# Seven block products in place of eight for the new gate of a GRU, in a graph network on one core

## Chip, cores and metric

One core of one Trainium2 chip. The metric is the device time of one execution in microseconds (us), lower is better; the time of a kernel is the median of its runs.

## What is computed

Four layers run over 128 graphs of 64 nodes with 256 features each, so over 8192 rows. Every layer adds its result to its input (`x = x + layer(relu(layernorm(x)))`). Layers 0 and 1 are graph attention (four heads, then one head), each ending in `elu`. Layer 2 is a relational convolution. Layer 3, where most of the work is, is a gated graph network of three steps:

```
for i in range(3):
    m = h @ weight[i]                      # messages
    a = adjacency applied to m             # sums over neighbours
    gi = a @ w_ih.T + b_ih;  gh = h @ w_hh.T + b_hh
    r = sigmoid(gi_r + gh_r)
    z = sigmoid(gi_z + gh_z)
    n = tanh(gi_n + r * gh_n)
    h = (1 - z) * n + z * h
```

All data are float32. For `r` and `z` the two matrix products may be added before anything else happens. For `n` they may not: `gh_n` is multiplied by `r` first, so its two halves (`gh_n` from h, `gi_n` from a) have to be kept apart.

## The kernel before

**Tiling.** The rows are split into 16 groups of 512 (four pairs of graphs). Features lie on partitions in two blocks of 128 (index `k` for inputs, chunk `c` for outputs), the 512 rows of a group lie along the free axis in two halves `S0` and `S1` of 256. A group passes attention twice, then the relational layer, then `before_recurrence` (layer norm and first neighbour sums), then the recurrence of three steps.

**Order of work.** Nothing runs in the order in which it is written. Class `Plan` records every operation with an assumed cost, the operations it depends on, and a job (`begin(name, start, end)`). `emit` then walks through an assumed time: of the operations that could start earliest on each engine, it takes the one with the earliest due time. The due time comes either from the job's own start and end (in proportion to what is left of the job) or, where the end is None, from the operations that follow. `LATENCY` is the assumed time from an engine's end to another engine's start. The order on each engine is fixed when the kernel is built. The recurrence of group g is due from `start + g * period`, and attention of later groups is fitted in between. In the first 115 us of the assumed time, waits of TensorE are filled with products of constants (`spare`, line 1315, into the bank `ni`).

**The recurrence** (`recurrence`, `class Chunk`). The products for `r` and `z` of one chunk use a scheme of seven block products where the plain way has eight (two input blocks by two output blocks by two halves of rows). It needs sums of weight blocks (`weight_sums`, made once into `wsum`) and sums of state blocks (`state_sums`, three or four POOL additions for each of h and a, into `hS` and `aS`). `mul(name, q, source)` is product number q from h (source 0) or a (source 1); it multiplies 128 x 128 weights with 256 columns. Products 1, 6, 5 and 3 are added up one after another in the PSUM bank `ry`. Between them ACT copies the partial sums that other outputs need (`m1_there`, `m16_there`, `m165_there`), so TensorE can't go on in that bank until the copy is done. Product 2 goes to `rm`, products 7 and 4 to `rz`. DVE adds those banks to the copies, ACT applies tanh (sigmoid is written with tanh).

**The n gate before.** `gate("nh", k)` and `gate("ni", k)` are plain: for each chunk two products of 512 columns into bank `nh` (from h) and two into `ni` (from a), eight for each step. ACT takes `nh` out with its bias into `t` (`nh_there`, 512 columns), DVE makes `(r + 1) * t` (`r_there`), then adds `ni` from PSUM (`n_there`), ACT applies tanh, POOL forms `d = h - n`, DVE finishes `d = (z + 1) * d` and `hnew = d / 2 + n` (`h_there`).

**After a step**, `back` transposes the new state on TensorE, `along` multiplies with the adjacency in 64 x 64 tiles, `state_sums` follows.

**Attention.** `values` takes the value columns out of PSUM on ACT and the few attention terms `es` on DVE; `aggregate_graphs` scales the result on DVE; `elu_add` takes the minimum with 0 on DVE and the exponential on ACT. Each has a switch `by_scalar` that gives the work to ACT; it is off for all groups (`g < 0`). `later_weights` prepares the weights of layers 2 and 3 in the early part, job "weights". All compute instructions are recorded by one helper, so in the profile they all have line 384 (line 605 where many products are one operation, `beside`).

PSUM has the banks `ry`, `rm`, `rz`, `nh` and `ni` of one tile each, which only the recurrence uses, and three for everything else (`mt` in the code; in the early part the first four of the five are lent out as well).

Of the kernel before, what the change touches and what calls it, by code (L numbers as in the profile page):

```python
# [8 lines left out]
F32 = mybir.dt.float32  # L9
I32 = mybir.dt.int32  # L10
AF = mybir.ActivationFunctionType
ALU = mybir.AluOpType
# [187 lines left out]
class Job:  # L200
# [3 lines left out]
    def __init__(self, start, end, after):  # L204
        self.start, self.end, self.after, self.left, self.length = start, end, after, 0, 0.0


class Plan:
# [3 lines left out]
    LATENCY = 164.2  # L212
# [54 lines left out]
    def emit(self):  # L267
# [20 lines left out]
        for op in reversed(self.ops):  # L288
            if op.job.end is None:
                op.due = min((t.due for t in op.then), default=1e9) - op.cost  # L290
            else:
                op.due = (op.job.end - (op.job.end - op.job.start) * op.tail / op.job.length) * 1e3
# [148 lines left out]
def kernel(  # L441
# [54 lines left out]
    wsum = nc.kept(const, [P, 1 + LAYERS, 3, D], F32, name="wsum")  # L496
    bi = nc.kept(const, [P, 6], F32, name="bi")
# [224 lines left out]
    def weight_sums(w, ws):  # L722

        r0, r1, z0, z1 = w[:, 0, :D], w[:, 1, :D], w[:, 0, D : 2 * D], w[:, 1, D : 2 * D]
        nc.gpsimd.tensor_tensor(ws[:, 0], z0, z1, ALU.add)
        nc.gpsimd.tensor_tensor(ws[:, 1], ws[:, 0], r0, ALU.subtract)
        nc.gpsimd.tensor_tensor(ws[:, 2], r1, ws[:, 1], ALU.subtract)
        nc.gpsimd.tensor_tensor(z0, r0, z0, ALU.subtract)

# [27 lines left out]
    def recurrence(work, psum, start, src, abd, store, in_parts=False):  # L757
# [16 lines left out]
        class Chunk:  # L774
# [3 lines left out]
            def __init__(self, c, i, hT, hnew):  # L778
                self.c, self.i, self.hT, self.hnew = c, i, hT, hnew
                self.banks, self.started = {}, set()  # L780
                self.r, self.t, self.z, self.d = (work.tile([P, T], F32, name=name) for name in "rtzd")
# [8 lines left out]
            def mul(self, name, q, source):  # L790

                w, m, ms = ((whh, self.hT, hS), (wc[:, self.i], aT, aS))[source]
                ws = wsum[:, (0, 1 + self.i)[source]]
                cs = slice(self.c * P, (self.c + 1) * P)
                zs = slice(D + self.c * P, D + (self.c + 1) * P)
                lhsT, rhs = {
                    1: (w[:, 0, cs], m[:, 0, S0]),
                    2: (w[:, 1, cs], m[:, 1, S0]),
                    3: (ws[:, 2, cs], m[:, 1, S1]),
                    4: (w[:, 1, zs], ms[:, 3]),  # L800
                    5: (ws[:, 0, cs], ms[:, 0]),
                    6: (ws[:, 1, cs], ms[:, 1]),
                    7: (w[:, 0, zs], ms[:, 2]),
                }[q]
# [4 lines left out]
                return 0.43  # L809

            def both(self, name, q):
                return self.mul(name, q, 0) + self.mul(name, q, 1)

            def gate(self, name, k):

                w, m = {"nh": (whh, self.hT), "ni": (wc[:, self.i], aT)}[name]
                ps, new = self.bank(name)
                f = 2 * D + self.c * P
                nc.tensor.matmul(ps, w[:, k, f : f + P], m[:, k, :], start=new, stop=not new)
                return 0.86  # L820

            def nh_there(self):
                nc.scalar.activation(self.t, self.banks["nh"], AF.Identity, bias=bh[:, 4 + self.c : 5 + self.c])

            def r_there(self, h):

                r, t = self.r[:, h], self.t[:, h]
# [6 lines left out]
                nc.vector.scalar_tensor_tensor(t, r, 1.0, t, op0=ALU.add, op1=ALU.mult)  # L834

            def n_there(self, h):
                t = self.t[:, h]
                nc.vector.tensor_tensor(t, t, self.banks["ni"][:, h], ALU.add)
                nc.scalar.activation(t, t, AF.Tanh, bias=bi[:, 4 + self.c : 5 + self.c])
                nc.gpsimd.tensor_tensor(self.d[:, h], self.hT[:, self.c, h], t, ALU.subtract)  # L840
# [16 lines left out]
            def h_there(self, h):  # L857
                d = self.d[:, h]
                nc.vector.scalar_tensor_tensor(d, self.z[:, h], 1.0, d, op0=ALU.add, op1=ALU.mult)
                nc.vector.scalar_tensor_tensor(  # L860
                    self.hnew[:, self.c, h], d, 0.5, self.t[:, h], op0=ALU.mult, op1=ALU.add
                )

        for i in range(LAYERS):
            last = i == LAYERS - 1
            hnew = work.tile([P, K, T], F32, name="hT")
            a = Chunk(0, i, hT, hnew)

            a.mul("ry", 1, 0)
            a.gate("nh", 0)  # L870
            if i > 0:
                aT = work.tile([P, K, T], F32, name="aT")
                if 0:
                    back(hT, hnat, 1)
                    along(psum, hnat, abd, aT, range(K))
                else:
                    along(psum, hnat, abd, aT, [0])
                state_sums(aT, aS, 0)
            a.mul("ry", 1, 1)
            a.m1_there()  # L880
            a.gate("ni", 0)
            if i > 0 and not 0:
                back(hT, hnat, 1)
            a.gate("nh", 1)
            a.nh_there()
            if i > 0:
                if not 0:
                    along(psum, hnat, abd, aT, [1])
                state_sums(aT, aS, 1)
            a.mul("rm", 2, 0) + a.mul("rz", 7, 0)  # L890
            a.mul("rm", 2, 1)
            a.r_there(S0)
            a.mul("rz", 7, 1)
            a.gate("ni", 1)
            a.n_there(S0)
            a.both("ry", 6)
            a.m16_there()
            b = Chunk(1, i, hT, hnew)
            b.both("rm", 2)
            a.both("ry", 5)  # L900
            a.m165_there()
            a.z_there(S1)
            b.gate("nh", 0)
            a.both("ry", 3)
            a.r_there(S1)
            a.n_there(S1)
            a.h_there(S1)
            a.both("rz", 4)
            a.z_there(S0)
            a.h_there(S0)  # L910

            b.gate("nh", 1)
            b.nh_there()
            b.both("ry", 1)
            b.m1_there()
            b.r_there(S0)
            b.both("rz", 7)
            b.both("ry", 6)
            b.m16_there()
            b.gate("ni", 0)  # L920
            b.both("ry", 5)
            b.m165_there()
            b.z_there(S1)
            hnat = work.tile([P, G, D], F32, name="hnat")
            back(hnew, hnat, 0, src if last else None)
            b.both("ry", 3)
            b.r_there(S1)
            b.gate("ni", 1)
            b.n_there(S0)
            b.n_there(S1)  # L930
            b.h_there(S1)
            b.both("rz", 4)
            b.z_there(S0)
            b.h_there(S0)
# [13 lines left out]
    with ExitStack() as s1:  # L948
# [148 lines left out]
        def attention(g, p0, n, layer, heads, we, pool):  # L1097
# [4 lines left out]
            wv, es = values(pool, psum, src, heads, we, g >= AHEAD, True, g < 0)  # L1102
# [51 lines left out]
            o = aggregate_graphs(pool, psum, t, wv, heads, g < 0)  # L1154
            elu_add(pool, src, o, nc.vector if g < 1 else nc.gpsimd, g < 0)
# [5 lines left out]
        def later_weights(prep):  # L1161
# [7 lines left out]
            weight_sums(whh, wsum[:, 0])  # L1169
            ihT = prep.tile([P, K, 3 * D], F32, name="ihT", tag="hhn")  # L1170
            transpose_blocks(psum, ihT, ihn, 6)
            for i in range(LAYERS):
# [12 lines left out]
                weight_sums(wc[:, i], wsum[:, 1 + i])  # L1185
# [49 lines left out]
        gru = Pool(None, 1, ("r3", "t3", "z3", "d3"))  # L1235
# [19 lines left out]
        nc.begin("weights", 18.0, 79.1)  # L1255
        later_weights(early)
        layers = (first_layer, second_layer, third_layer)
        start, period = 93.6, 83.8
# [274 lines left out]
```

## Time and profile before

| what | value |
|---|---|
| time, median of 3 runs | 1435.51 us (1435.34 to 1436.21) |
| the profiled execution, its own time | 1434.47 us |
| its span, first to last instruction | 1432.5 us |
| share of clock granted to TensorE | 0.998 |
| TensorE busy (matmul) / weight load | 1412.5 us / 973.6 us |
| DVE / ACT / POOL busy | 1041.5 / 778.7 / 597.7 us |
| first product of the recurrence starts | 113.0 us |
| last product that isn't of the recurrence starts | 1324.9 us |

How to read it. PE is TensorE (matmul), PEld its weight loads, DVE is VectorE, ACT is ScalarE, POOL is GpSimd. A float32 matmul instruction leaves two records in the trace, so "x384" matmul records are 192 products. A group is named "output tile <- input tiles". Matmul durations reach from the start to the end of the pipeline and overlap each other; the spacing of the starts is what a product costs in a stream. The kernel has a second path (`general`) for inputs out of bounds, which isn't run; its instructions are in the listing but not in the trace.

### The profile page before, as it was taken

The page shows a single profiled execution, that of the slowest core. Times are in us where ns is not written, and L with a number is a line of the kernel's source. Part 1 is how long each engine was busy: PE and PEld are TensorE (multiplying, and loading weights), DVE is VectorE, ACT ScalarE, POOL GpSimd, SP SyncE. Part 2 cuts the span into 40 slices and gives each one's busy share as a digit, 9 for nine tenths or more (in the row PEclk, how much of TensorE's full clock was granted, in tenths as well). Part 3 has the DMA queues.
Part 4 walks back from the last instruction along what each step waited for, and adds up shares of the span by engine and source line. Part 5 has one row for each costly group of instructions (what it writes and reads, how often), then busy time and mean ns, then how long its engine had stood idle before and what let it go on. Part 6 is the DMA issues. An engine that isn't in the chain of part 4 may idle for free.

```text
span 1432.5 us, 28063 instructions
## 1 busy us (share of the span) xinstructions
PE 1412.5 (99%) x9779; PEld 973.6 (68%) x9779; DVE 1041.5 (73%) x2745; ACT 778.7 (54%) x1853; POOL 597.7 (42%) x744
## 2 busy tenths in 40 slices
PE   9999999999999999999999999999999999999997
PEld 9676676666667666666766666676666667666664
DVE  5568688686867878686887868688686868774544
ACT  3654655555565565556555555655655555554543
POOL 1424624534434453443445344344534434452422
PEclk9999999999999999999999999999999999999999
DMA  7010221222223122222312222231212222110000
GB/s 214 19 27 24 38 60 30 47 53 52 60 43 75 28 51 54 52 60 44 77 25 51 54 52 60 43 76 27 46 39 48 46 42 58 25 34 15 16 16 18
DMA packets 299421, 67.91 MB, mean 47 GB/s; under 512 B 274696, under 2 KB 297480, under 8 KB 299272
## 3 DMA queue, kind: packets, MB, share of 16 engines
q1 hardware_dynamic: 298712, 65.50, 21.7%
q8 instruction: 81, 1.33, 0.4%
q10 hardware_dynamic: 560, 0.52, 0.1%
q14 instruction: 68, 0.56, 0.1%
HBM read 28.06 MB, written 8.53 MB: 26 GB/s over the span
## 4 chain that ended last, share of the span: by engine, by line
PE 88%; DVE 4%; SPq 3%; ACT 3%; DMA 1%; issue 1%; POOL 1%; DVEq 0%; POOLq 0%; ACTq 0%
PE ry L384 22%; PE mm L384 16%; PE rz L384 11%; PE ni L384 11%; PE nh L384 10%; PE rm L384 5%; PE tp L384 4%; PE mm L605 3%; SPq L384 3%; PE tp L605 2%; PE ni L1315 2%; DVE d L384 1%; POOL d L384 1%; DVE hT L384 1%; DMA t<-row 1%
## 5 line engine op out<-in xcount | busy, mean ns | idle before, releaser
L384 POOL TENSOR_TENSOR d<-hT,t 128x256 f32<-128x256 f32 x192 | 151.9, 798 | 487.7 <-ACT t L384 486.8
L384 PE MATMUL ni<-aT,wc 128*128 128x512 f32 x384 | 194.1, 592 | 0.0
L384 PE MATMUL nh<-hT,whh 128*128 128x512 f32 x384 | 193.8, 593 | 0.2 <-DVE hT L384 0.2
L384 ACT ACTIVATE z<-z,brz 128x256 f32<-128x256 f32 x192 | 97.4, 507 | 155.9 <-DVE z L384 155.3
L384 DVE SCALAR_TENSOR_TENSOR d<-z,d 128x256 f32<-128x256 f32 x192 | 127.2, 669 | 58.1 <-POOL d L384 45.2
L384 POOL TENSOR_TENSOR hS<-hT 128x256 f32<-128x256 f32 x96 | 73.9, 770 | 175.5 <-PE ry L384 136.3
L384 ACT COPY z<-ry 128x256 f32<-128x256 f32 x192 | 71.2, 371 | 126.4 <-PE ry L384 91.2
L384 DVE SCALAR_TENSOR_TENSOR t<-r,t 128x256 f32<-128x256 f32 x192 | 98.0, 511 | 50.2 <-ACT r L384 44.5
L384 DVE TENSOR_TENSOR z<-rz,z 128x256 f32<-128x256 f32 x192 | 80.2, 418 | 59.1 <-PE rz L384 46.6
L384 PE MATMUL rz<-hS,whh 128*128 128x256 f32 x384 | 119.5, 393 | 1.1 <-DVE z L384 1.0
L384 PE MATMUL mm<-wl,hT 128*128 128x512 f32 x248 | 118.1, 598 | 0.0
L384 PE MATMUL ry<-hS,wsum 128*128 128x256 f32 x384 | 115.9, 383 | 0.8 <-ACT z L384 0.8
L384 PE MATMUL rz<-aS,wc 128*128 128x256 f32 x384 | 115.6, 383 | 0.0
L384 PE MATMUL ry<-aS,wsum 128*128 128x256 f32 x384 | 114.2, 379 | 0.0
L384 ACT ACTIVATE hn<-xg,var,rstd 128x256 f32<-128x256 f32 x200 | 107.1, 592 | 9.9 <-DVE var L384 9.8
L384 ACT ACTIVATE t<-t,bi 128x256 f32<-128x256 f32 x192 | 93.8, 502 | 19.8 <-DVE t L384 19.2
L384 PEld LDWEIGHTS ry<-hS,wsum 128*128 128x128 f32 x384 | 70.0, 190 | 47.0 <-issue 32.0
L384 DVE BATCH_NORM_STATS2 st<-xg 128x6 f32<-128x256 f32 x256 | 98.5, 413 | 3.2 <-DMA xg<-in_x_dram 2.5
L384 DVE SCALAR_TENSOR_TENSOR hT<-d,t 128x256 f32<-128x256 f32 x192 | 91.9, 485 | 6.1
L384 POOL TENSOR_TENSOR rstd<-var,mhalf 128x4 f32<-128x4 f32 (+1 forms) x70 | 68.7, 984 | 56.4 <-DVE var L384 47.4
L384 PEld LDWEIGHTS nh<-hT,whh 128*128 128x128 f32 x384 | 70.1, 190 | 27.3 <-issue 17.4
L384 PEld LDWEIGHTS ry<-aS,wsum 128*128 128x128 f32 x384 | 73.0, 190 | 22.7 <-issue 10.3
(203 smaller groups left out, 3227.6 us busy)
## 6 DMA issues: line engine op xcount, KB each, us to landing
hT<-hn SPq DMA_DIRECT2D x896, 32.0 KB
xg<-in_x_dram SPq DMA_DIRECT2D x15, 512.0 KB
out_dram<-hnat SPq DMA_DIRECT2D x15, 512.0 KB
t<-row SPq DMA_DIRECT2D x28, 256.0 KB
at<-in_adj_dram SPq DMA_DIRECT2D x64, 32.0 KB
eg<-in_adj_dram SPq DMA_DIRECT2D x64, 32.0 KB
ag<-in_adj_dram SPq DMA_DIRECT2D x16, 128.0 KB
t<-row SPq DMA_DIRECT2D x28, 64.0 KB
```

Source lines behind the costliest of these rows:

```text
L384: return do(*[real(a) for a in args], **{k: real(v) for k, v in kwargs.items()})
L605: nc.nc.tensor.matmul(*[real(x) for x in product], start=True, stop=True)
L1315: nc.spare = lambda: nc.nc.tensor.matmul(pause, warm, warm, start=True, stop=True)
```

## The change

1. **n by seven products.** The new function `part_of_n` makes both chunks of `gh_n` (source 0) or of `gi_n` (source 1) from seven products of 256 columns, 14 for each step. The two chunks take the place that the r and z blocks have in `Chunk`, with their own weight sums `nsum`. Products 1, 6, 5 and 3 go to bank `nh` with ACT copies in between, 2 to `rm`, 7 and 4 to `ni`, and DVE adds (`plus`) the latter three times. Source 0 ends in `t`, source 1 in `hnew`, except that chunk 0, half S1 of source 1 is read from PSUM.
2. **The gate arithmetic** follows (`gate_n`): `tc` plus `hnew` are mostly two SBUF operands; the difference h - n goes into `hnew` and no longer into an own tile `d`. `r`, `z`, `t` are now tiles of both chunks.
3. **Order in which a step is written:** neighbour sums, `part_of_n(0)`, r of chunk 0, `part_of_n(1)`, then n, z, the new state and `back` of chunk 0, then the same of chunk 1.
4. **ACT** takes `es`, the scaling of the one-head attention and elu's minimum (as `Relu(-x)`, `Exp(-x)`) for all groups (`g < 16`).
5. **The plan:** `LATENCY` 164.2 to 177.99; jobs without an end get due times by `spread * (cost + LATENCY)`; "weights" and all jobs of groups 0 and 1 have no end now; `start`, `period` and due times move a little; the filling of waits stops when the first recurrence bank is taken.

The core of the diff:

```diff
-    LATENCY = 164.2
+    LATENCY = 177.99
...
-                op.due = min((t.due for t in op.then), default=1e9) - op.cost
+                op.due = 1e9
+                for t in op.then:
+                    late = 0.0 if t.engine == op.engine else self.LATENCY
+                    op.due = min(op.due, t.due - op.job.spread * (op.cost + late))
...
+    nsum = nc.kept(const, [P, 1 + LAYERS, 3, P], F32, name="nsum")
...
-            def gate(self, name, k):
-
-                w, m = {"nh": (whh, self.hT), "ni": (wc[:, self.i], aT)}[name]
-                ps, new = self.bank(name)
-                f = 2 * D + self.c * P
-                nc.tensor.matmul(ps, w[:, k, f : f + P], m[:, k, :], start=new, stop=not new)
-                return 0.86
...
+        def part_of_n(source, i, hT, to):
+
+            w, m, ms = ((whh, hT, hS), (wc[:, i], aT, aS))[source]
+
+            def mul(ps, q, start, stop):
+                lhsT, rhs = operands(q, w, nsum[:, (0, 1 + i)[source]], *NN, slice(0, P), m, ms)
+                nc.tensor.matmul(ps[:, S0], lhsT, rhs, start=start, stop=stop, skip_group_check=True)
+
+            def there(c, h, ps):
+                if source == 0:
+                    nc.scalar.activation(to[:, c, h], ps[:, S0], AF.Identity, bias=bh[:, 4 + c : 5 + c])
+                else:
+                    nc.scalar.copy(to[:, c, h], ps[:, S0])
+
+            def plus(c, h, ps):
+                engine = nc.vector if source == 0 else nc.vector
+                engine.tensor_tensor(to[:, c, h], ps[:, S0], to[:, c, h], ALU.add)
+
+            y = psum.tile([P, T], F32, name="nh")
+            mul(y, 1, True, False)
+            there(0, S0, y)
+            m2 = psum.tile([P, T], F32, name="rm")
+            mul(m2, 2, True, True)
+            plus(0, S0, m2)
+            mul(y, 6, False, False)
+            there(1, S0, y)
+            m7 = psum.tile([P, T], F32, name="ni")
+            mul(m7, 7, True, False)
+            mul(y, 5, False, False)
+            there(1, S1, y)
+            plus(1, S1, m7)
+            mul(m7, 4, False, True)
+            plus(1, S0, m7)
+            mul(y, 3, False, True)
+            return y
...
+            def gate_n(c, h, y):
+                tc, new = t[:, c, h], hnew[:, c, h]
+                nc.vector.scalar_tensor_tensor(tc, r[:, c, h], 1.0, tc, op0=ALU.add, op1=ALU.mult)
+                nc.vector.tensor_tensor(tc, tc, y[:, S0] if (c, h) == (0, S1) else new, ALU.add)
+                nc.scalar.activation(tc, tc, AF.Tanh, bias=bi[:, 4 + c : 5 + c])
+                nc.gpsimd.tensor_tensor(new, hT[:, c, h], tc, ALU.subtract)
...
-            wv, es = values(pool, psum, src, heads, we, g >= AHEAD, True, g < 0)
+            wv, es = values(pool, psum, src, heads, we, g >= AHEAD, True, g < 16)
...
-            o = aggregate_graphs(pool, psum, t, wv, heads, g < 0)
-            elu_add(pool, src, o, nc.vector if g < 1 else nc.gpsimd, g < 0)
+            o = aggregate_graphs(pool, psum, t, wv, heads, g < 16)
+            elu_add(pool, src, o, nc.vector if g < 1 else nc.gpsimd, g < 16)
...
-        nc.begin("weights", 18.0, 79.1)
+        nc.begin("weights", 18.0, 0 or None)
...
-        start, period = 93.6, 83.8
+        start, period = 84.23, 83.53
...
-                    nc.begin((g, p0, i), at[i], at[i + 1], [users[i]] if i in users and not spare else [])
+                    end = None if g < 2 else at[i + 1]
+                    nc.begin((g, p0, i), at[i], end, [users[i]] if i in users and not spare else [])
...
-            nc.spare = lambda: nc.nc.tensor.matmul(pause, warm, warm, start=True, stop=True)
+            nc.spare = lambda: psum.early and nc.nc.tensor.matmul(pause, warm, warm, start=True, stop=True)
```

## The prediction

> **What bounds the kernel now.** I began with the first part of the page and the chain of waits, which ask the same question from two sides: which engine is never free, and whose work the end hangs on.
>
> ```profile
> PE 1412.5 (99%) x9779; PEld 973.6 (68%) x9779; DVE 1041.5 (73%) x2745; ACT 778.7 (54%) x1853; POOL 597.7 (42%) x744
> ...
> PE 88%; DVE 4%; SPq 3%; ACT 3%; DMA 1%; issue 1%; POOL 1%; DVEq 0%; POOLq 0%; ACTq 0%
> ```
>
> TensorE is busy for 99% and 88% of the last-ending chain is its products. A busy matmul row alone proves little, since its bars overlap, so I looked at starts in the timeline of some steady microseconds.
>
> ```profile
> 300.20 0.60 PE L384 MATMUL rz<-hS,whh 128*128 128x256 f32 x2
> 300.63 0.59 PE L384 MATMUL rz<-aS,wc 128*128 128x256 f32 x2
> 301.06 0.27 PE L384 MATMUL tp<-ident,hT 128*128 128x128 f32 x1
> 301.17 1.02 PE L384 MATMUL nh<-hT,whh 128*128 128x512 f32 x2
> 302.03 0.59 PE L384 MATMUL ry<-hT,whh 128*128 128x256 f32 x2
> ```
>
> A product of 256 columns is followed 0.43 us later by the next, one of 512 columns (301.17 to 302.03) 0.86 us later, whatever tile follows. By the start times of the whole trace the medians are 0.431 and 0.859 us. Both are streams without a hole. The three stretches of the span, cut at the first product of the recurrence and at the last one of another layer, show where that holds:
>
> ```profile
> 0.00:113.00 113.00, 110.94 (x842) 85.96 (x842) 66.85 (x240) 56.81 (x151) 36.14 (x61) 1.00 0.31 83
> 113.00:1325.00 1212.00, 1207.55 (x8342) 823.43 (x8338) 923.42 (x2388) 671.97 (x1590) 523.80 (x633) 1.00 0.23 47
> 1325.00:1432.50 107.50, 93.98 (x608) 64.20 (x600) 51.19 (x118) 49.94 (x113) 37.74 (x51) 0.97 0.07 17
> ```
>
> After the length come PE, PEld, DVE, ACT and POOL. In the middle PE has 4.5 us of 1212 free; DVE, next, is at 76%. At the end, where only the last recurrence is left, PE lacks some 13 us. At the start PE looks busy but a third of that is filling:
>
> ```profile
> L1315 PE MATMUL ni<-warm 128*128 128x128 f32 x318 | 41.7, 286 | 1.1 <-DVE warm L1313 1.1
> L384 PE MATMUL ni<-aT,wc 128*128 128x512 f32 x384 | 194.1, 592 | 0.0
> L384 PE MATMUL nh<-hT,whh 128*128 128x512 f32 x384 | 193.8, 593 | 0.2 <-DVE hT L384 0.2
> ```
>
> 318 records are 159 filling products of 0.22 us, 35 us. The other two rows are the products that the change replaces. So: TensorE's own work sets the time, except in about 35 us of early waits and some 13 us at the end.
>
> **What the Trainium skill says.** "Perfetto Trace Analysis", section "Identifying the Most-Contended Engine", warns that matmul busy time is not a measure of how full TensorE is, because matmuls are pipelined. This trace agrees: bars of 592 ns mean, starts 429 ns apart; therefore I price by starts. "TensorE: Matmul & The Clock Gate", section "Back-to-back issue gap", gives N/2.4 + 2.5 ns warm. With N twice the float32 columns that is 215.8 and 429.2 ns for one record; the medians here are 215.5 and 429.2. So halving a product halves its price, with 2 ns lost, and the shorter one isn't held up by its weight load (190 ns). "SBUF — State Buffer", section "SBUF: two separate sides", says that a DVE instruction with two SBUF inputs and a POOL instruction exclude each other for a whole instruction. The trace agrees: `t<-r,t` takes 384 ns at least and 954 at most between 600 and 700 us.
>
> **Part 1, products.** Removed for each of 48 steps (16 groups by 3): eight products of 512 columns, 8 x 0.859 = 6.87 us. Added: 14 of 256, 14 x 0.431 = 6.03 us. In all 384 x 0.859 = 329.8 against 672 x 0.431 = 289.6: **-40.1 us** of TensorE. Since PE is full before and after in the middle stretch, all of it is on the path there. At the end the chain of the last recurrence decides in part, so a share of 3 of the 48 steps, 2.5 us, could be lost. Switches between 64-row and 128-row products, which cost PE some 0.1 to 0.3 us each, are 324 in both built orders: nothing.
>
> **Part 2, turns of a bank.** New are the copies between products in `nh`, twice per step. TensorE must not write on before ACT has read. Queued behind such a product on PE is everything else, as the order is fixed. What a turn takes is seen near the end: the last product into `ry` before one starts at 1419.26, its second record 0.22 later at 1419.48, and the next product in that bank at 1420.32, 0.84 us after that record's start, of which 0.22 are its own stream: 0.62 with a copy of 371 ns. An evacuation with bias (about 466 ns, from `r<-ry,brz`) gives 0.72. It costs nothing when other products lie in between. In the built order of after, nine of ten turns of `nh` have 1.29 us or more of other products between them, so the cover is mostly there. But all banks together have 191 revisits with under 1.0 us of cover, against 106 before, and the lines of the PE listing with a wait grow from 1829 to 2162 (18%). In the trace of before, what 128-row records took beyond the stream adds up to 29 us between 120 and 1340. Growing with the waits that is +5, growing with the thin revisits (+80%) +24. I take **+8**, nearer to the first, because most thin revisits still have 0.4 us or more of cover. If the cover were gone: see the third rival.
>
> **Part 3, DVE.** Gone: 192 `t<-t,ni` x 0.412 = 79; 124 `es` copies, 18.6; 64 of the one-head `o`, 26.9; `hn<-o`, 31.4. Added: 288 `plus` from PSUM x 0.415 = 119.5; 144 additions of two SBUF operands at the price of `t<-r,t`, 0.511 = 73.6 (425 ns when free, 669 with POOL often in the way); 48 from PSUM, 19.8. Net +57, so 1098 of about 1395 us, 79%. **ACT:** gone 96 x 0.689 = 66; added 192 x 0.466 + 144 x 0.371 + 124 x 0.16 (from copies of 256 and 512 at 371 and 585 ns, extrapolated to a few columns) + 64 x 0.466 + 28 x 1.058 + 8 x 0.632 = 227. Net +161: 940 us, 67%. **POOL** stays: the 192 differences only change their target, and 16 small sums of weights fall into the early part. SP's queue has the same 1254 lines. All of this lies beside TensorE: **0** on the path, price of a lost cover in the second rival. `hnew` is held a little longer than before; three `hT` tiles exist and I price that at 0, with up to 3 us in the range.
>
> **Part 4, early work.** The built order holds 121 filling products for 159, so 38 x 0.22 = 8.4 us fewer, and the first recurrence product follows 54.8 us of 128-row work instead of 71.9; the rest of the weights moves behind it, where it fills waits. But filling now stops at that product, and holes after it aren't seen in the listing. Bounds -9 to +3; I take **-6**. `spread = 3.0` does nothing, as those jobs keep an end.
>
> **Part 5, the end.** After the last r product two plain `ni` products no longer stand before the wait for the new state. Before, the wait was 2.59 us (1422.4 to 1425.0) behind one 0.86 us product less: **+1**.
>
> **Sum.** -40.1 + 8 - 6 + 1 = -37. The profiled execution took 1434.47 us (span 1432.5 and 2.0 around it): 1397.4. The median of the runs is 1.0 above that execution: 1398.
>
> **Rivals.** (a) *TensorE stays full*, as summed: **1398**, own range 1388 to 1406 from parts 2, 4 and 5. For it: the first three views. Chance 0.62. (b) *DVE becomes the bound in its dense stretches.* In the steady part two windows of ten microseconds stand out:
>
> ```profile
> 630.00:640.00 10.00, 10.00 (x96) 6.61 (x94) 9.24 (x19) 5.30 (x12) 5.83 (x5) 1.00 0.09 16
> 640.00:650.00 10.00, 10.00 (x62) 5.55 (x62) 9.33 (x31) 5.67 (x13) 6.67 (x10) 1.00 0.01 2
> ```
>
> 18.6 of 20 us. DVE's +57 spread over 16 periods is 3.6 for each 83.4 us, so 0.9 here: 19.4, in a stretch that TensorE would now do in 19.4. If DVE needs the 1.4 us of slack it has now, each period loses 1.4, in all 23: 1421; with half of it lost, 1409. I take **1415** (1406 to 1425). Against it: 77 of the 156 us taken from DVE lie in attention, as part of these windows does. Chance 0.26. Smaller gains still, 1425 to 1432, as when the order hides holes: 0.05. (c) *The bank `nh` turns without cover.* Eight turns a step at 0.72 us. From 46 / 48 / 0.72 = 1.3 bare turns a step on, the gain is eaten. Two a step are 69 us: 1434.5 - 46 + 69 = **1458**. Against it: the nine of ten with 1.29 us. Chance 0.05. (d) That the change brings nothing measurable (within 0.2%, 2.9 us, which is about what a measurement here can tell from no change): 0.02.
>
> So faster 0.62 + 0.26 + 0.05 = 0.93, same 0.02, slower 0.05. The range takes in all of (a), below it the early bound and a stall cost at nothing, and two thirds of (b): 1384 to 1418.
>
> **What would show it.** PE at 98% or more and 672 products into `nh`, `ni` and `rm` for n; filling near 242 records; the middle stretch about 2.5 us shorter for each group. Wrong if PE shows waits on ACT for `nh` (c), if DVE stands at 9.8 of 10 in windows where PE has holes (b), or if holes follow the first recurrence product (part 4).

## The result and the profile after

| what | before | after |
|---|---|---|
| time, median | 1435.86 us (4 runs) | 1490.33 us (4 runs, 1485.94 to 1496.56) |
| the profiled execution, its own time / span | 1434.47 / 1432.5 us | 1496.56 / 1494.8 us |
| granted share of the TensorE clock | 0.998 | 0.973 |

The kernel became slower: ratio 1.0381 (95% interval 1.0342 to 1.0419). The forecast was 1398. The four runs of after lie 10.6 us apart and follow the granted clock (1485.94 us at 0.985, 1489.52 at 0.981, 1491.14 at 0.976, 1496.56 at 0.973), and the profiled one is the slowest of them. These are the first lines of the page of after: busy time and instructions of each engine, then the 40 slices of TensorE and of its clock.

```profile
PE 1401.0 (94%) x10279; PEld 1094.8 (73%) x10279; DVE 1097.1 (73%) x2805; ACT 914.0 (61%) x2321; POOL 623.9 (42%) x760
...
PE   9999788989999898999999999999999999999987
...
PEclk9998899999999999999999999999999999999999
```

PE was 99% busy and is now 94%. Over the whole span no other engine is near its limit: DVE has the same 73% as before. So no engine took over as the bound everywhere. TensorE has less to do and waits more.

**Where the 62.3 us of span come from.** I added up the starts of all matmul records of both traces. A hole is a distance between starts that exceeds the product's own stream by 0.35 us or more.

| term | before | after | difference |
|---|---|---|---|
| products that n replaces, 384 x 0.859 against 672 x 0.431 | 329.8 | 289.6 | -40.1 |
| filling (318 records, 242 records) | | | -8.4 |
| holes of TensorE | 14.8 | 98.8 | +84.0 |
| products that stream at half the clock, excess | 0.1 | 29.2 | +29.1 |
| gaps under 0.35 us | 45.7 | 43.4 | -2.3 |
| sum | | | +62.3 |

By count and price the products saved what they were to save: the stream still takes 0.431 us for 256 columns. The saving came back nearly three times over as holes and as half clock.

**By stretch.** These windows cut the span at the start of the first recurrence, at the start of the third, and at the start of the last, which runs alone. The columns are length, PE, PEld, DVE, ACT, POOL, granted clock, DMA share, GB/s. Before:

```profile
113.00:280.50 167.50, 165.78 (x1166) 113.34 (x1163) 128.66 (x339) 93.62 (x223) 75.12 (x92) 1.00 0.19 39
280.50:1357.10 1076.60, 1072.14 (x7414) 731.03 (x7413) 812.91 (x2094) 595.74 (x1407) 464.94 (x564) 1.00 0.23 47
1357.10:1426.10 69.00, 63.15 (x364) 43.20 (x363) 32.55 (x74) 32.55 (x74) 21.47 (x29) 1.00 0.04 13
```

After:

```profile
83.90:302.10 218.20, 192.88 (x1416) 146.45 (x1416) 147.76 (x389) 131.10 (x345) 87.15 (x108) 0.93 0.17 33
302.10:1415.50 1113.40, 1060.73 (x7875) 831.36 (x7876) 858.52 (x2166) 699.48 (x1763) 480.04 (x562) 0.98 0.22 46
1415.50:1488.30 72.80, 64.41 (x410) 52.94 (x408) 42.42 (x94) 36.99 (x89) 26.50 (x36) 0.98 0.04 12
```

The third recurrence starts at 302.1 us and not at 280.5, though the first begins 29 us earlier: +21.6. The 13 groups between take +36.8, the last recurrence +3.8. In the middle PE now has 52.7 us free (1113.4 - 1060.7), against 4.5. DVE's share is 77% (858.5 of 1113.4) and was 76%.

**One hole, followed.** TensorE's waits in the middle stretch of after, listed by what ended them, begin with the following (engine and tile that waited, what released it, us in total, times, longest).

```profile
PE ry L388 <- ACT z L388: 22.2, 8, 2.8
PE ry L388 <- DVE hT L388: 5.9, 3, 2.7
PE tp L388 <- DVE hT L388: 5.0, 4, 2.0
```

In the same list of before the longest row has 0.9 us. The 8 waits of 2.8 us are one hole, in eight groups some 86 us apart (672, 757, 843 and so on). This is the timeline of that hole at 757 us, and below it the end of the same hole in an earlier group:

```profile
754.54 0.41 DVE L388 SCALAR_TENSOR_TENSOR hT<-z,hT 128x256 f32<-128x256 f32 x1
...
757.08 0.59 PE L388 MATMUL rz<-aS,wc 128*128 128x256 f32 x2
757.19 0.41 DVE L388 TENSOR_TENSOR o<-mm,rec 128x256 f32<-128x256 f32 x1
757.52 0.93 DVE L388 TENSOR_TENSOR t<-t,hT 128x256 f32<-128x256 f32 x1
758.37 0.41 DVE L388 TENSOR_TENSOR o<-mn,rec 128x256 f32<-128x256 f32 x1
758.70 0.41 DVE L388 TENSOR_TENSOR z<-rz,z 128x256 f32<-128x256 f32 x1
759.03 0.41 DVE L388 SCALAR_TENSOR_TENSOR hT<-z,hT 128x256 f32<-128x256 f32 x1
759.06 0.96 POOL L388 TENSOR_TENSOR hT<-hT,t 128x256 f32<-128x256 f32 x1 [0.90 <-ACT t L388]
759.37 0.94 DVE L388 SCALAR_TENSOR_TENSOR hT<-hT,t 128x256 f32<-128x256 f32 x1
759.84 0.49 ACT L388 ACTIVATE z<-z,brz 128x256 f32<-128x256 f32 x1
...
760.45 0.67 PE L388 MATMUL ry<-hT,whh 128*128 128x256 f32 x2 [2.78 <-ACT z L388]
760.57 1.28 DVE L388 SCALAR_TENSOR_TENSOR hT<-z,hT 128x256 f32<-128x256 f32 x2
...
761.53 1.06 PE L388 MATMUL nh<-hT,whh 128*128 128x256 f32 x2
```

```profile
409.23 0.41 DVE L388 SCALAR_TENSOR_TENSOR hT<-hT,t 128x256 f32<-128x256 f32 x1
...
409.79 0.77 PE L388 MATMUL ry<-hT,whh 128*128 128x256 f32 x1 [2.67 <-DVE hT L388]
```

PE has issued the last product of a step at 757.08 and needs the new state for the next one. The view puts the wait down to ACT's `z`, but that isn't what TensorE waits for. In all eight of these holes, in the one at 409.79 and in one of the early part (133.96), the product starts 0.14 to 0.15 us after the end of DVE's `hT<-hT,t`, the last instruction of the new state (here 759.37 + 0.94 = 760.31). In the last two, `z` had ended 1.7 us before; in the eight it ends 0.02 to 0.03 us after DVE by coincidence, and DVE's next `hT<-z,hT` starts at 760.57, when TensorE has already gone on.

By the order of the source, the state that TensorE needs is the first half of chunk 0. Its other DVE instruction, `hT<-z,hT`, was done at 754.95, so `hT<-hT,t` could have run 4.4 us earlier. In DVE's fixed order it stands behind work for the other half and for chunk 1 and behind two scalings `o` of attention. Two of these DVE instructions take longer, with POOL at work beside them: the new addition of two SBUF operands, `t<-t,hT`, 0.93 us and not 0.39, and `hT<-hT,t` itself, 0.94 and not 0.41. No product of attention was placed here to cover the 2.8 us. The last PE row at 761.53 shows the next loss: two records of 256 columns take 1.06 us from start to end, and 0.59 before the hole.

```profile
757.30:760.40 3.10, 0.37 (x2) 0.00 (x0) 3.10 (x7) 1.98 (x5) 1.79 (x3) 1.00 0.28 45
760.40:763.80 3.40, 3.35 (x41) 2.51 (x42) 3.40 (x6) 2.05 (x4) 2.25 (x3) 0.62 0.33 54
```

In the first of these windows of after DVE works 3.10 of 3.10 us; in the ten before 760.4 it works 9.97, and PE 7.27. In the second the granted clock is 0.62. Of nine holes of 2.8 to 2.95 us in the middle groups, eight are followed by such a stretch at half clock. The nine make 26 of the 58 us of holes in the middle.

### The profile page after: what moved, and what is told of

Its sections match the earlier page's. It is cut to its first block, busy times and chain, and to the rows that moved or that the text cites. A ratio compares the mean times of both kernels' runs of the same rounds, so it can differ in the third digit from the quotient of the medians.

```text
span 1494.8 us, 29550 instructions
## 1 busy us (share of the span) xinstructions
PE 1401.0 (94%) x10279; PEld 1094.8 (73%) x10279; DVE 1097.1 (73%) x2805; ACT 914.0 (61%) x2321; POOL 623.9 (42%) x760
## 5 line engine op out<-in xcount | busy, mean ns | idle before, releaser
L388 POOL TENSOR_TENSOR hT<-hT,t 128x256 f32<-128x256 f32 x192 | 149.7, 784 | 607.6 <-ACT t L388 494.2
L388 DVE SCALAR_TENSOR_TENSOR hT<-z,hT 128x256 f32<-128x256 f32 x192 | 112.6, 599 | 15.8 <-POOL hT L388 11.5
L388 ACT ACTIVATE t<-nh,bh 128x256 f32<-128x256 f32 x192 | 91.1, 475 | 44.2 <-PE nh L388 27.7
L388 DVE SCALAR_TENSOR_TENSOR hT<-hT,t 128x256 f32<-128x256 f32 x192 | 103.9, 564 | 0.8
L388 POOL TENSOR_TENSOR hS<-hT 128x256 f32<-128x256 f32 x96 | 88.2, 920 | 30.1 <-DVE hT L388 19.8
L388 DVE BATCH_NORM_STATS2 st<-xg 128x6 f32<-128x256 f32 x256 | 92.1, 408 | 5.4 <-POOL xg L388 2.9
L388 PE MATMUL ry<-hT,whh 128*128 128x256 f32 x192 | 62.6, 409 | 33.6 <-ACT z L388 22.2
L388 POOL TENSOR_TENSOR aS<-aT,aS 128x256 f32<-128x256 f32 x96 | 75.3, 784 | 37.8 <-ACT aT L388 37.4
L388 PE MATMUL rm<-hT,whh 128*128 128x256 f32 x288 | 88.9, 391 | 1.8 <-DVE hT L388 1.5
L388 POOL TENSOR_TENSOR hS<-hT,hS 128x256 f32<-128x256 f32 x96 | 77.2, 804 | 31.5 <-DVE hT L388 30.9
```

Of the source, the lines that this page charges most:

```text
L388: return do(*[real(a) for a in args], **{k: real(v) for k, v in kwargs.items()})
```

## The experiments

Two theories stand against each other. One: the change is slower because of one of its parts, the products with their turns and additions, ACT's work, or the plan. The rival: no part has a price of its own. Before is full because its order, fixed at the build, was fitted to its own constants, and any edit throws the order again. Time is the median of the runs, and the ratio is to runs of before made beside them; holes and half clock are from the profiled execution, counted as above.

| run | products | ACT | plan | time, us | ratio to before [95%] | holes / half clock, us |
|---|---|---|---|---|---|---|
| before | | | | 1435.86 | 1 | 14.8 / 0.1 |
| act_only | | x | | 1469.37 | [1.0208, 1.0267] | 48.2 / 3.2 |
| plan_only | | | x | 1492.12 | [1.0361, 1.0421] | 73.6 / 7.7 |
| act_plan | | x | x | 1495.10 | [1.0408, 1.0446] | 83.5 / 7.2 |
| products_only | x | | | 1524.85 | [1.0568, 1.0681] | 98.7 / 33.3 |
| products_act | x | x | | 1495.19 | [1.0387, 1.0448] | 89.6 / 21.7 |
| products_plan | x | | x | 1547.83 | [1.0737, 1.0832] | 119.8 / 49.7 |
| after | x | x | x | 1490.33 | [1.0342, 1.0419] | 98.8 / 29.2 |

**The three parts, in all pairings.** ACT's part is three switches. The plan's part is part 5 of the change, put in or taken back as a whole; the products' part is parts 1 to 3.

```diff
-            wv, es = values(pool, psum, src, heads, we, g >= AHEAD, True, g < 0)
+            wv, es = values(pool, psum, src, heads, we, g >= AHEAD, True, g < 16)
...
-    LATENCY = 164.2
+    LATENCY = 177.99
...
-        start, period = 93.6, 83.8
+        start, period = 84.23, 83.53
```

> Only the ACT part of the change on the kernel before. Theory 1: slower than before by 10 to 40 us with holes at the end of a step. Theories 2 and 3: within 5 us of before, 1431 to 1441.

> Only the plan part of the change (LATENCY, due times, start, period, end of filling) on the kernel before. If the plan part is a cause of its own: 1450 to 1490 with a first recurrence of 100 us or more. If it only suffers from the products: 1425 to 1440.

> The ACT part and the plan part of the change, without the products (the last corner of the three parts). If parts add up: 1435 + 34 + 57 = 1526. If the products cost something of their own in the whole change: below 1490, and the last recurrence takes about 69 us as in every kernel with the order of a step of before. If the whole loss comes from the ACT and plan parts and the products gain their 40 us: 1510 to 1530.

> Only the products of the change on the plan and the ACT work of before. Theory 2 (bank turns and DVE work of the products): slower than before, 1450 to 1490. Theories 1 and 3: TensorE stays full, 1395 to 1410, groups of about 81 us.

> The change without its plan part: LATENCY, due times, start, period and filling as before; products and ACT part as changed. Theory 3 (plan): the first two recurrences take 84 us each again and the time falls to 1430 or less. Theory 1 (ACT) and theory 2 (bank turns): still above 1460, with holes in the steady groups of 6 us or more.

> The change without its ACT part: es, one-head scaling and elu's minimum go back to DVE for all groups; products and plan as changed. Theory 1 (ACT, with the Relu and Exp of 1.04 us each for the attention, delays the z and state of a step, so TensorE has a hole of 2.9 us at the end of a step in each group, and each such hole brings 3.4 us at half clock): the steady groups fall from 85.7 to about 81.5 us, time 1425 or less. Theory 2 (the new turns of the banks and the added DVE work of the products make the holes): time stays within 1475 to 1500. Theory 3 (the new due times starve TensorE): time stays, 1475 to 1500, the first recurrence again about 119 us long.

Measured: the table. Every part alone is slower, and so is every pair. The parts don't add up: act_only is +34 and plan_only +56, their sum 1526, but act_plan takes 1495. The products cost +89 alone (1524.85 - 1435.86), +26 beside ACT's part, +56 beside the plan's, and -5 beside both, which is within the spread of after's runs. A part with a price of its own would show about the same number four times, unless one part hides another.

No single theory of the forecasts came through. ACT as the cause (theory 1) fits act_only but not products_plan, which was to fall to 1425 and took 1548. The plan as the cause (theory 3) fits plan_only but not products_act, which was to fall to 1430 and took 1495. The products (theory 2) fit products_only in direction, but act_only and plan_only are slow without them. The 1495 of act_plan lies between its forecasts.

plan_only has every instruction of the calculation as before, and its middle stretch is 47.5 us longer (the second stretch below is that of act_only). ACT's part takes work off DVE, the second busiest engine, and leaves the products as they were:

```profile
291.00:1415.10 1124.10, 1087.67 (x7415) 732.62 (x7416) 816.66 (x2091) 597.43 (x1405) 483.88 (x570) 1.00 0.22 45
```

```profile
277.70:1390.60 1112.90, 1084.50 (x7416) 732.40 (x7416) 780.12 (x1938) 639.20 (x1576) 465.08 (x566) 1.00 0.22 46
```

In act_only DVE has 33 us less to do than in before (812.9), ACT 43 more, PE the same records, and the stretch is 36 us longer. Total load on the engines doesn't explain it. But load isn't ruled out where the seven products are: there ACT's part made the kernel faster in both pairs, by 30 us (products_only to products_act) and by 57 (products_plan to after), and without the products it cost 34 and 3.

**after_plain: the step order of after, with n by eight plain products.** ACT's work and the plan are those of after.

```diff
-        def part_of_n(source, i, hT, to):
+        def plain_n(source, c, i, hT, to):
...
+            for k in range(K):
+                nc.tensor.matmul(y, w[:, k, f : f + P], m[:, k, :], start=(k == 0), stop=(k == K - 1))
+            if source == 0:
+                nc.scalar.activation(to[:, c], y, AF.Identity, bias=bh[:, 4 + c : 5 + c])
```

> The changed kernel with its order of a step, its ACT part and its plan, but plain n products: 4 of 512 columns into nh, 4 into ni for each step, taken out as in the kernel before. TensorE has 40 us more to do. Theory C (order of a step, or the plan): still slow, 1470 or more. Theories A and B (what the seven products bring along): 1432 to 1450 in spite of the 40 us.

Measured: 1474.41 us [1.0238, 1.0297], with holes of 59.1 and 8.4 us at half clock. It has 40 us more products than after and is 16 us faster, but still slow, as theory C (the order of a step, or the plan) said. The last recurrence is the cleanest place to compare, since no attention is left to be placed in it:

```profile
1398.70:1465.80 67.10, 62.47 (x367) 43.99 (x366) 31.91 (x75) 32.30 (x74) 21.09 (x29) 1.00 0.04 13
```

With plain products in the old order this stretch took 68.7 to 69.3 us in before, in both variants of LATENCY, and with ACT's part, the plan's or both. The new order of a step makes it 67.1. With seven products it took 70.7 to 72.8 in all six kernels that keep them whole. There the seven-product form loses by itself.

**after_no_turns, after_no_plus, after_no_both: what in that form costs.** The first leaves out that the partial sums come from the bank: ACT reads the state or the neighbour sums in place of `nh`, so TensorE needn't wait for it. The second leaves out DVE's six additions per step. The third leaves out both. None of the three computes n.

```diff
-                    nc.scalar.activation(to[:, c, h], ps[:, S0], AF.Identity, bias=bh[:, 4 + c : 5 + c])
+                    nc.scalar.activation(to[:, c, h], m[:, c, h], AF.Identity, bias=bh[:, 4 + c : 5 + c])
...
-                    nc.scalar.copy(to[:, c, h], ps[:, S0])
+                    nc.scalar.copy(to[:, c, h], m[:, c, h])
...
-                engine.tensor_tensor(to[:, c, h], ps[:, S0], to[:, c, h], ALU.add)
+                pass
```

> The changed kernel, but ACT's six copies between the n products of a step read the state or the sums and not the bank, so no product in the bank nh waits for a copy. ACT's work, DVE's work and the products stay; the n gate's value is left wrong (the partial sums never leave the bank). Theory A (bank turns make the holes of TensorE): holes and half-clock time mostly go, 1400 to 1425. Theory B (the additions on DVE make them) and theory C (the order of a step: all n products early, so too little to cover the end of a step): 1475 or more.

> The changed kernel without DVE's six additions for n in each step (288 in all, 119 us of DVE); the products into rm and ni for n are made and never read, so the n gate's value is left wrong. Theory B (DVE): 1400 to 1430. Theories A and C: a gain of under 20 us, 1470 or more.

> The changed kernel with ACT's copies between the n products reading state instead of the bank, and without DVE's six additions of a step (the n gate's value is left wrong): seven products for n with nothing else that they bring along. Theory D: the 40 us of TensorE are there, but its order is as unfitted as the others: 1450 to 1490. Theories A and B together (turns and additions make the holes): 1395 to 1425.

Measured: 1497.43 [1.0398, 1.0458], 1535.14 [1.0639, 1.0742] and 1478.46 us [1.0254, 1.0354]. The last recurrence, in that order:

```profile
1419.40:1488.30 68.90, 62.77 (x407) 51.87 (x408) 41.09 (x95) 36.42 (x89) 25.14 (x34) 1.00 0.04 13
```

```profile
1455.50:1523.40 67.90, 61.44 (x401) 50.45 (x400) 33.26 (x76) 36.76 (x89) 21.73 (x29) 1.00 0.04 13
```

```profile
1406.20:1473.00 66.80, 60.83 (x394) 49.15 (x393) 33.22 (x75) 36.56 (x89) 20.99 (x29) 1.00 0.04 13
```

From 72.8 in after the turns are worth 3.9 us and the additions 4.9, but not in sum: without both it is 6.0. Of after's 72.8 us, 3.4 are at half clock, behind three holes of 0.8 to 1.1 us; that costs at most 1.7 us and is gone in all three. It leaves 2.2 us for the turns and 3.2 for the additions over three steps, 0.7 and 1.1 us a step. The products are 0.84 us a step shorter, but this gain hardly shows here: without turns and additions the stretch is only 0.3 us below that of plain products in the same order (66.8 against 67.1). TensorE isn't full in it (60.8 of 66.8 us); the chain of the step decides. So this stretch shows what turns and additions add to that chain, and not what fewer products are worth where TensorE is full.

In the whole kernel no forecast by turns or additions came true (theories A and B, 1395 to 1430), and the second run says the opposite of a price: taking away 288 additions of 0.42 us made it 45 us **slower** than after. The middle stretch of that run takes 1158 us. It was not clean as an ablation, since the builder places all other work anew.

**before_165, before_168: nothing but one constant of the plan.**

```diff
-    LATENCY = 164.2
+    LATENCY = 165.2
```

> The kernel before with LATENCY 165.2 instead of 164.2, nothing else: the same operations, only the assumed time between engines is one nanosecond longer. Theory D (the order is fitted to its constants: any edit gives another order with holes in TensorE's work, whatever the edit does): 1450 to 1475. Theory E (the order is robust, and the products, ACT and plan parts cost what they cost by themselves): 1434 to 1440.

> The kernel before with LATENCY 168.2 instead of 164.2, nothing else. Theory D: 1450 to 1475, not the same as with 165.2 and in no order of the constants. Theory E: 1434 to 1440.

Measured: 1445.66 us [1.0054, 1.0100] for 165.2, and 1439.61 [1.0021, 1.0055] for 168.2. The same instructions with an assumed latency larger by 1 ns cost about 11 us, and by 4 ns about 5 (the ratios times 1435.9). In before_165 the holes double, from 14.8 to 29.0 us; this is its middle stretch:

```profile
282.30:1368.40 1086.10, 1071.52 (x7410) 732.46 (x7409) 818.48 (x2093) 593.20 (x1407) 470.34 (x563) 1.00 0.23 47
```

PE's busy time is that of before (1072.1), the length 9.5 us more. So the full TensorE of before belongs to one order, and a near one has holes. But the forecast of theory D, 1450 to 1475, was too high for both, and 1439.61 lies in the range of theory E. A small change of a constant costs 5 to 11 us, not the 34 to 112 of the table.

**after_retuned: the instructions of after, other constants of the plan.** The constants were picked by building many sets and taking the order with the fewest holes by the plan's assumed times.

```diff
-    LATENCY = 177.99
+    LATENCY = 182.65
...
-        start, period = 84.23, 83.53
+        start, period = 90.06, 84.66
...
-                units = [(0, G, (82.1, 127.0, 176.1, 238.0))]
+                units = [(0, G, (85.54, 104.64, 165.05, 244.16))]
...
-                end = start + g * period - 26.98
+                end = start + g * period - 26.84
```

> The changed kernel with other constants of the plan (LATENCY 182.65, spread 1.84, start 90.06, period 84.66, due times of groups 1 and 2 moved), found by trying some 600 sets and taking the one whose order holds the fewest holes by the plan's own assumed times. Operations unchanged. Theory D: below the 1490 of the changed kernel by 15 us or more, 1445 to 1475, still above before since no set was found without holes. Theories A, B: within 10 us of 1490.

Measured: 1456.56 us [1.0122, 1.0181]. That recovers 34 of the 55 us with no instruction of the calculation changed, as theory D said.

```profile
91.20:273.70 182.50, 174.64 (x1345) 135.19 (x1344) 133.14 (x367) 119.80 (x310) 83.47 (x107) 0.99 0.20 40
273.70:1377.80 1104.10, 1065.58 (x7882) 834.34 (x7881) 845.49 (x2170) 694.28 (x1774) 472.38 (x564) 0.98 0.23 46
```

The early part ends at 273.7 us, 28.4 before after's and 6.8 before before's. The middle is only 9.3 us shorter than after's, which is no more than after's runs differ among themselves, and 27.5 longer than before's. The hole of 2.8 us is gone: none in this middle reaches 2 us. But TensorE still waits for the new state from DVE, in shorter pieces; this is the longest row of its list:

```profile
PE tp L388 <- DVE hT L388: 26.6, 25, 1.7
```

**after_old_early: after with before's early work** (due times, the end of "weights", the filling).

```diff
-        nc.begin("weights", 18.0, 0 or None)
+        nc.begin("weights", 18.0, 79.1)
...
-        start, period = 84.23, 83.53
+        start, period = 93.6, 83.53
...
-            nc.spare = lambda: psum.early and nc.nc.tensor.matmul(pause, warm, warm, start=True, stop=True)
+            nc.spare = lambda: nc.nc.tensor.matmul(pause, warm, warm, start=True, stop=True)
```

> The changed kernel with the early part of the plan as before: start 93.6, due times of groups 0 and 1 and of the weights from their jobs' ends, filling up to 115 us of assumed time. LATENCY, period, the later due times, products and ACT stay as changed. If the early plan (first recurrence 30 us sooner, filling cut off there) costs what the comparison of the two traces shows: the first two recurrences end near 280 us instead of 302, time 1460 to 1475. If those 20 us come from the products as well: the first two end at 295 or later, time 1480 or more.

Measured: 1476.09 us [1.0270, 1.0319]. The third recurrence starts at 284.3 us, 17.8 before after's, near the first forecast (the time is 1 us above its range); the middle takes 1116.1 (1113.4 in after). So the early part of the plan, put back as a whole, accounts for most of the +21.6, and for nothing of the middle. Where it goes in after:

```profile
133.96 1.19 PE L388 MATMUL ry<-hT,whh 128*128 128x256 f32 x2 [2.82 <-DVE hT L388]
...
182.17 1.18 PE L388 MATMUL tp<-ident,hn 128*128 128x128 f32 x3 [7.74 <-ACT hn L388]
```

The filling has ended, as the first recurrence bank is taken at 83.9 us; behind it the other early work no longer covers the waits. The end of the filling alone isn't the cause, since after_retuned ends it in the same way. The second hole lies in this window, where DVE works 18.1 of 20 us and TensorE's clock falls to 0.74:

```profile
172.00:192.00 20.00, 10.95 (x44) 5.83 (x44) 18.14 (x57) 9.93 (x22) 8.55 (x9) 0.74 0.12 20
```

**plain_order_tuned: before, with only after's order of a step** and its tiles, plain products, DVE's and ACT's work as in before, and constants picked in the same way.

```diff
-    LATENCY = 164.2
+    LATENCY = 163.49
...
-        start, period = 93.6, 83.8
+        start, period = 95.80, 83.93
```

> The kernel before (plain n products, its ACT work, its rule for due times) with only the new order of a step, and constants of the plan found by trying some 1,600 sets (LATENCY 163.49, start 95.8, period 83.93, due times moved). The last recurrence should take 67 us instead of 69 as in the run with plain products. If fitted constants are what holds TensorE full: 1425 to 1436, last recurrence 67 us. If the kernel before can't be matched by a new order even with fitted constants: 1445 or more.

Measured: 1436.29 us in 15 runs, 1433.93 for before beside them (ratio [1.0008, 1.0024]). The last recurrence takes 67.0 us, 2.0 less than in before, but the middle is 9.4 longer and the early part 4.5 shorter:

```profile
276.00:1362.00 1086.00, 1073.62 (x7421) 737.15 (x7420) 844.11 (x2094) 600.45 (x1406) 470.42 (x567) 1.00 0.23 47
1362.00:1429.00 67.00, 62.33 (x365) 43.53 (x364) 32.79 (x75) 32.44 (x74) 21.14 (x29) 1.00 0.04 13
```

It is 0.16% slower than before, within the 0.2% that the prediction called nothing measurable. So a new order of a step can be made as full as the old one with constants of its own. No version that I ran beats before.

## Why the prediction was wrong

**The failing step** is the last sentence of part 1: "Since PE is full before and after in the middle stretch, all of it is on the path there". The saving of 40.1 us of products was right, and so was their price. That PE is full *after* was assumed, not derived. It was read off before's trace as if it held for any order; plan_only, with the same calculation, has 47.5 us more in the middle. The measured holes of after are 98.8 us and the excess at half clock 29.2. The 1490 lies above every rival of the prediction, (c) with its 1458 included.

**Part 2** (+8) looked at the turns of one bank, where it found cover. Waits of PE on ACT for `nh` are not among the long ones in the middle, so rival (c), with two bare turns a step, isn't what happened there. In the last recurrence, where no cover is left, turns took 0.7 us a step and additions 1.1. The stall term missed the other places: the end of a step, where the new state is awaited, and the early part.

**Part 3** had the sizes of DVE right, 1097.1 against 1098 us, and ACT's 26 us too high, 914.0 against 940. Here are three of its rows:

```profile
L388 DVE TENSOR_TENSOR t<-t,hT 128x256 f32<-128x256 f32 x144 | 75.6, 533 | 0.6
L388 DVE TENSOR_TENSOR hT<-ni,hT 128x256 f32<-128x256 f32 x96 | 40.2, 419 | 9.1 <-PE ni L388 5.7 <-ACT hT L388 2.6
L388 ACT ACTIVATE t<-nh,bh 128x256 f32<-128x256 f32 x192 | 91.1, 475 | 44.2 <-PE nh L388 27.7 <-DVE hT L388 13.7 <-DVE mv L388 1.6
```

533 ns against 511 predicted, 419 against 415, 475 against 466. "All of this lies beside TensorE: **0** on the path" failed. At 757 us, `o`, `t<-t,hT` and other work stand in DVE's queue ahead of the new state, and TensorE waits for that.

**Rival (b)** named the engine that TensorE waits for in that hole, and its sign came: DVE works 9.97 of 10 us where PE has the hole. It put the loss at 0.7 to 1.4 us per period where 2.8 was seen, and left out the half clock. DVE's load alone doesn't hold as the cause of the whole loss: its share in the middle is 77% after 76%, less load on DVE made the middle longer (act_only by 36 us over before, after_no_plus by 45 over after), and after_retuned has the same instructions with 26.6 us of waits for the new state in pieces under 2 us. A dense DVE and an order that puts the new state late act together here; the runs don't part them.

**Part 4** (-6) had the direction wrong for these constants: +21.6 up to the start of the third recurrence, of which 17.8 go with the old early work. It could be had, as after_retuned is 6.8 us ahead of before there. The prediction did name holes after the first recurrence product as what would prove it wrong, and those came.

**Part 5** (+1): the last recurrence, of which it is a part, took +3.8 where the parts together gave -2.5 of products and +1. Part 1 had said that these 2.5 us could be lost.

**Half clock** had no term. "TensorE: Matmul & The Clock Gate", section "Part 1: The HAM clock gate", says that TensorE falls to half rate after an idle window of about 3.4 us. In the traces less idleness is enough. All 16 stretches at half clock in after begin on one grid of 3.413 us (675.91, 761.24, 846.57: 25 steps apart), and in the grid window before each TensorE was idle for 1.77 us or more. Of the 397 other windows one reached that (1.81 us), and the rest stayed under 1.63. These are a hole in one window with half clock behind it, and the ninth hole of 2.8 us, which fell across two windows (PE 1.95 and 1.85 us busy) and had none:

```profile
757.83:761.24 3.41, 0.79 (x5) 0.72 (x6) 3.41 (x8) 2.76 (x4) 1.75 (x3) 1.00 0.33 53
761.24:764.65 3.41, 3.41 (x42) 2.64 (x41) 2.95 (x4) 1.75 (x5) 2.65 (x3) 0.50 0.29 49
1273.24:1276.65 3.41, 1.95 (x38) 1.37 (x30) 3.38 (x11) 1.67 (x4) 1.57 (x3) 1.00 0.31 51
1276.65:1280.06 3.41, 1.85 (x28) 1.38 (x32) 3.41 (x8) 2.73 (x4) 1.89 (x3) 1.00 0.33 54
```

A hole thus costs itself and, where it fills about half of such a window, part of the 3.4 us after it: 29 us on 84 of new holes.

**What stays open.** For the early part the cause is shown by an edit that undoes it. For the middle, +36.8 us, it is shown that instruction load alone doesn't explain it, that other constants break up the repeated hole, and what TensorE waits for in it. That they recover 9.3 us is not clear of the spread of after's runs, and it is not shown what part of the rest the seven-product form makes unavoidable. Of the kernels with seven products only after_no_both had a run of groups at about 83.0 us (from the start of one recurrence to the next; 83.4 in before), and then two of 104.7 and 91.8. Whether a wider search for constants would find an order of after as full as that of before wasn't tried.

## What to carry to other kernels

An engine that is 99% busy under an order fixed at build time shows that this order fits, not that the engine will stay full after an edit. Before pricing a saving on it, ask how the order was made, and see what moving its constants does to the time: here 1 ns of an assumed latency moved it by 0.8% and the new constants and due times of plan_only by 3.9%, so each edit of the instructions had to be priced with a new throw of the order of such a size. And where a view names what ended a wait, compare several occurrences of it: here the engine named was not the one waited for. Judge an instruction-level idea in a stretch with no other work to place, here the last recurrence: the new order of a step gained 2 us there, while the seven products took 3.6 to 5.7 us longer than plain ones in the same order. Such a stretch shows what an edit adds to the chain of a step; what less work is worth where TensorE is full has to be measured there.

## What was unexpected of the hardware

Half clock doesn't need a hole of 3.4 us. In after all 16 stretches, 83.6 us in all, follow a window of a fixed grid of 3.413 us in which TensorE idled for 1.77 us or more, so several small holes can do it and a hole of 2.8 us across two windows need not. The middle of after_retuned has 11 such stretches, though none of its holes reaches 2 us. In the 17 traces no window with less than 1.4 us of idle time was followed by half clock, and every one with more than 2 us was; between these values both occur. In after the stretches cost 29.2 us of streaming.

The addition of two SBUF operands on DVE took 0.93 us beside POOL's instruction at 757.52 and 0.39 when free, and it stood ahead of the new state that TensorE waited for.
